# Up-projection pieces read raw in every pass, and two gate searches moved, in a one-core fp32 attention and feed-forward kernel

## The chip, the cores and the metric

The kernel runs on one core of one Trainium2 chip. The metric is the device time of one execution in microseconds (us), the median of the runs shown. Five engines take part, each with an instruction queue of its own that it works off in order: TensorE (PE, with its weight loads shown as PEld), VectorE (DVE), ScalarE (ACT), GpSimd (POOL) and SyncE (SP). In this kernel SP and POOL issue the DMAs.

## The reference

Two residual blocks over x of shape (2, 2048, 1024), all in fp32. The second is the one that matters here:

```python
x = x + attention(_layernorm(x), Wqkv, bqkv, Wo, bo)      # D = 256, one head
hs = _layernorm(x)
logits = hs @ gate_w                                       # 1024 -> 8
routing_weights, _ = jax.lax.top_k(logits, 2)
h = relu(hs @ up_w) ** 2                                   # 1024 -> 2048
shared_out = h @ down_w                                    # 2048 -> 1024
expert_out = (hs @ fc1_w) @ expert_w                       # 1024 -> 512 -> 512
moe_out = expert_out * routing_weights.sum(-1, keepdims=True)
x = x + layernorm(shared_out + moe_out @ fc2_w) * ln_gamma + ln_beta
```

## The kernel before

**Arithmetic.** Every fp32 product is made of three TensorE matmuls on a split of both operands into a rounded half ("hi", written by an ACT cast) and a remainder ("lo", written by a DVE subtract): hi·hi, lo·hi, hi·lo (`Pass3.add`, L131). The feed-forward block works on pairs of token blocks of 512 rows in four passes, b = 0 to 3 (called passes 1 to 4 here). Each pass is an "up" stage (hidden states times up_w and fc1_w) and a "down" stage (times down_w and fc2 folded with the expert weights). Each stage is done with seven Strassen-like products, p1 to p7, of ten chunks (NK = 10; chunks 0 to 7 of a product belong to up_w or down_w, 8 and 9 to the latent part). A chunk is one weight piece of 128x1024 (hi in the first 512 columns, lo in the second) and twelve matmuls.

**Order of up.** `up_order` lists the 70 chunks of a stage. In passes 2 to 4 it begins p1,0; p1,1; p2,0; p1,2; p2,1; p1,3; p2,2 ... up to chunk 19, p2,9. So chunk number m is p1,i for m = 2i-1 and p2,i for m = 2i+2, and the last is chunk 19. Then come p4, p6, p5, p3 and p7, the last in the order 0 to 5, 8, 9, 6, 7. In pass 1 the first four chunks are p1,0 to p1,3 and the mixing begins after them.

**Weight pieces.** `next_piece` runs a pipeline in program order: while chunk m is emitted, `end_piece` emits the DVE subtract of chunk m+2 (L938), `cast_piece` the ACT cast of chunk m+3 (L931), and `stage` the SP load of chunk m+4. A piece is loaded in one of three ways:

- already split, 512 KB, from a copy in HBM (`w<-w_p`, L898), with no cast and no subtract. The copy was written by POOL from an earlier pass (`w_p<-w`, L941) if `keep` was true;
- raw, 256 KB, straight from up_w or fc1_w (`raw<-in_L_ffn_up_w_dram`, L905), into a tile of the pool `spp`, which has four buffers and also holds the activations of the down stage. A raw load therefore waits for the subtract of the raw piece four loads before it;
- raw, 256 KB, from a sum of quarters or from the copy `lead` (p1,0 to p1,3) into the second half of the weight tile (`w<-wt`, `w<-wt_lead`, L905). There are seven weight tiles.

For p1 and p2 of up, `keep` is true in pass 1 for the even pieces. So passes 2 to 4 load ten of these twenty pieces split and ten raw.

**What else stands in these chunks.** After the matmuls of a chunk ACT takes the result out of PSUM (`copy` for p1 at L1239, `relu` for p2 at L1140, with a `square` over each pair at L1143). In odd chunks below 17, `out_step` finishes output rows of the pass before: on DVE `write` (L1094, L1095), on ACT `second` (L274, L275) and `first` (L262, L263), on POOL a store and an accumulating load of beta, on SP a load `res<-x` (L1078). In chunks 11, 13, 15 and 17, `split_x` prepares X["p4"]: an ACT cast `xh` (L150) and, with `split_late`, a DVE subtract `xl` (L151) that is emitted at the start of the next chunk.

**The gates.** The gate logits are summed out of products `pg` (L987), each eight matmuls appended to a chunk by `gate_part`. The first gate is complete after p2,0, the second after its product with X["p7"] in p3,8. X["p7"] is made by `split_x` in p3,1, p3,3, p3,5 and p3,7. `Gate.largest` (L1005 to L1017, DVE) searches the two largest logits of each row, `send` writes the sums to HBM and `spread` loads them back broadcast as `rwb`, both on POOL. `rwb[0]` is first used at p2,8 (L1242), `rwb[1]` at p7,8 (L1266). The small tiles `ga`, `gs`, `gtt`, `gtop`, `rwb` and the throw-away outputs `junk` of `second` and `first` come from one pool, `half`, with four buffers.

The order on every queue is the program's: the stage stands in `tc.manual_schedule()`.

Of the kernel before, what the change touches and what calls it, by code (L numbers as in the profile page):

```python
# [25 lines left out]
def kernel(  # L26
# [69 lines left out]
    def f32(t):  # L96
        return t.bitcast(FP)
# [55 lines left out]
    def flush():  # L153
        for f in late_ops:
            f()
        late_ops.clear()
# [185 lines left out]
    def piece(pr, c, n, sl):  # L342
        return tuple(v.rearrange("p (c n) -> p c n", n=n)[:, c, sl] for v in pr)
# [18 lines left out]
    def as_piece(t, s):  # L362

        return t.rearrange("p (c n) -> p c n", n=P) if s == 0 else t
# [510 lines left out]
    def direct(s, p, i):  # L875

        return s == 0 and p in ("p1", "p2", "p3") and (p, i // LEAD) != ("p1", 0)

    def source(s, p, i):
        q = RIGHT[p]  # L880
        if s == 0 and isinstance(q, tuple):
            parts = quarter(s, *q) if direct(s, p, i) else [lead]
        else:
            parts = tsum[s, q]
        t, j = (parts[0], i) if i < HU // P else (parts[1], i - HU // P)
        return t[:, ts(j, P)].rearrange("(c p) i -> p c i", p=P) if s == 0 else t[ts(j, P), :]

    def stage():


        b, s, p, i = pieces.pop(0)
        if len(pieces) < LATE and early:
            staged.append((early.pop(0), None, None))
            return
        n_w[0] += 1
        w = (wk if n_w[0] % 7 else wv).tile([P, 2 * W], FR, tag="w", name="w")
        if (s, p, i) in kept:
            nc.sync.dma_start(out=w.bitcast(FP), in_=kept[s, p, i])  # L898
            staged.append((w, None, None))
            return  # L900
        if direct(s, p, i):
            raw = spp.tile([P, 2 * W], FP, tag="sp", name="raw")[:, 0:W]
        else:
            raw = f32(w)[:, W : 2 * W]
        nc.sync.dma_start(out=as_piece(raw, s), in_=source(s, p, i))  # L905

        if s == 1 and p in ("p3", "p7", "p4"):
            keep = b == 2 and p == "p4" and i >= NK - LATE  # L910
        elif s == 0 and p in ("p1", "p2"):

            keep = b == 0 and i % 2 == 0
        else:
            keep = b == 1 or i % 2 == 0
        staged.append((w, raw, (s, p, i) if keep else None))
# [27 lines left out]
    def next_piece():  # L944

        while (pieces or staged or cast) and len(ready) < 3:
            if cast:
                end_piece()
            while pieces and len(staged) < 2:
                stage()  # L950
            if staged and not cast:
                cast_piece()
        return ready.pop(0)
# [3 lines left out]
    def acc_bank(name):  # L957
        n_bank[0] += 1
        return bank(psb if n_bank[0] % 3 == 2 else psa, name)
# [179 lines left out]
    def relu(o, v):  # L1139
        nc.scalar.activation(o, v, AF.Relu)  # L1140
# [4 lines left out]
    def relu_square(v):  # L1145
        relu(v, v)
        square(v)

    t1, later = xts, []
    with tc.manual_schedule():  # L1150
        for b in range(NBB):
# [6 lines left out]
            def h_at(name, i, n=1):  # L1158

                if i < HU // P:  # L1160
                    key, q = (name, i // 4), i % 4
                else:
                    key, q = (name in ("11", "12"), "l"), i - HU // P
                    q += 2 * (name in ("12", "21"))
                if key not in h:
                    h[key] = unit(f"h{b}", FP)
                return h[key][:, ds((q + 1 - n) * W, n * W)]
# [53 lines left out]
                nc.gpsimd.dma_start(out=gamma_sb, in_=ln_gamma.partition_broadcast(P))  # L1221
            rwb, acc = [None, None], {}
            n_bank[0] = 1
            for m, (p, i) in enumerate(UPS[b]):
                flush()
                w = next_piece()
                while later:
                    relu_square(later.pop())
                if p != "p2":
                    acc[i] = Pass3(acc_bank("pu"), NCC // 2)  # L1230
                ps = acc[i].ps
                if p == "p2":
                    acc[i].more()
                for c in range(NCC // 2):
                    acc[i].add(piece(w, c, P, slice(0, P)), piece(X[p], c, W, slice(0, W)))
                lat, pair = i >= HU // P, i % 2 and i < HU // P
                c22, c21 = h_at("22", i), h_at("21", i) if m >= 2 * NK else None
                if p == "p1":
                    nc.scalar.copy(c22, ps)  # L1239
                elif p == "p2":  # L1240
                    if lat:
                        add(h_at("11", i), ps, rwb[0], ALU.mult)  # L1242
                    else:
                        relu(h_at("11", i), ps)
                        if pair:
                            square(h_at("11", i, 2))
                elif p == "p4":
                    nc.scalar.copy(c21, ps)
                elif p == "p6":
                    add(c22, ps, c22, ALU.subtract)  # L1250
                    add(c21, c21, c22, ALU.subtract)
                elif p == "p5":
                    add(c22, c22, ps, ALU.add)
                elif p == "p3":
                    c12 = h_at("12", i)
                    add(c12, c22, ps, ALU.add)  # L1256
                    if lat:
                        add(c12, c12, rwb[0], ALU.mult)
                    elif pair:
                        relu(h_at("12", i, 2), h_at("12", i, 2))  # L1260
                        square(h_at("12", i, 2))
                else:
                    add(c21, c21, ps, ALU.add)
                    add(c22, c22, ps, ALU.subtract)
                    if lat:
                        add(c21, c21, rwb[1], ALU.mult)  # L1266
                        add(c22, c22, rwb[1], ALU.mult)
                    elif pair:
                        relu_square(h_at("21", i, 2))
                        later.append(h_at("22", i, 2))  # L1270

                if m % 2 and m < 17:
                    out_step()
                if b == 0 and m in (0, 1, 2, 3, 4, 6, 7, 8, 9, 10, 11):
                    norm2.step()
                if b == 0 and m < NB:
                    split_x(x_t[0], 1, m, X["p2"], split_late)
                if b == 0 and m % 2 == 0 and 24 <= m < 24 + 4 * NK:
                    j = m // 2 - 12
                    copy_step((1, j // NK), j % NK)  # L1280

                m4 = 10
                if m == m4:
                    x_t[1] = norm2.x
                    X["p4"] = new_x()
                if m > m4 and (m - m4) % 2 and (m - m4) // 2 < NB:
                    split_x(x_t[1], 1, (m - m4) // 2, X["p4"], split_late)
                elif m >= 2 * NK and p != "p7":
                    n = {"p4": "p6", "p6": "p5", "p5": "p3", "p3": "p7"}[p]
                    if i == 1:  # L1290
                        X[n] = new_x()
                    if i % 2 and i < 2 * NB:
                        if p == "p4":
                            sums_x(x_t, i // 2)
                        r_, f_ = PLACE[n]
                        split_x(x_t[r_], f_, i // 2, X[n], split_late)

                if (p, i) == ("p1", 0 if b else 4):
                    ga = half("ga")[:SQ, :]
                    nc.scalar.copy(ga, gate_part(X["p1"], 0))  # L1300
                elif (p, i) == ("p2", 0):
                    gs = half("gs")[:SQ, :]
                    add(gs, ga, gate_part(X["p2"], 1), ALU.add)
                    gt = Gate(gs)
                elif (p, i) == ("p4", 1):
                    add(ga, ga, gate_part(X["p4"], 1), ALU.add)
                elif (p, i) == ("p3", 8):
                    add(ga, ga, gate_part(X["p7"], 0), ALU.subtract)
                    gt = Gate(ga)
                if m == 11 or (p, i) == ("p3", 9):  # L1310
                    gt.largest()
                elif m == 12 or (p, i) == ("p7", 0):
                    gt.send()
                elif m == 14 or (p, i) == ("p7", 2):
                    rwb[p == "p7"] = gt.spread()
                if p == "p7" and (len(UPS[b]) - m) in (9, 7, 5, 3, 1):
                    step_s()
# [18 lines left out]
            for j, p in enumerate(("p1", "p2", "p6", "p5", "p3", "p7", "p4")):  # L1336
# [41 lines left out]
                if late:  # L1378
                    last_w = [next_piece() for _ in range(late)]
                    both = unit("last")  # L1380
                    while len(sp) < late:
                        i = len(sp) + len(sp_cast) - late + 2
# [78 lines left out]
```

## Time and profile before

| what | value |
|---|---|
| median of 3 runs | 2328.39 us (2327.54 to 2328.46) |
| the profiled execution: its own time | 2327.81 us |
| its span, first to last instruction | 2326.0 us |
| granted TensorE clock | 0.998 |
| PE busy | 2303.7 us, 99% of the span |
| DVE, ACT, POOL busy | 67%, 50%, 13% |
| DMA moved | 557.31 MB, mean 240 GB/s |

The profile is of one execution. A busy PE in it is a PE with a matmul in flight. The up stages of the four passes begin at about 755, 1145, 1536 and 1925 us. A list of waits names who waited for whom, the total in us, how many times, and the longest. A timeline row is: start, duration, engine, line, operation, tile written <- tiles read, count, and in brackets the idle time before it with what ended that.

### The profile page before, as it was taken

To read this page: it belongs to the slowest core of one execution; us is meant where nothing else is said; L and a number is where in the kernel's file an instruction comes from. 1 tells how busy PE (TensorE), PEld (TensorE's weight loads), DVE (VectorE), ACT (ScalarE), POOL (GpSimd) and SP (SyncE) were. 2 spreads that over 40 slices of the span, in tenths; PEclk is the share of its full clock that TensorE was granted. 3 is DMA by queue.
4 is the path that set the end of the run, shared out by engine and by line. 5 is a ranking of instruction groups with operands and counts; after the bars stand their busy time and mean duration, and the time that the engine had idled before them with its cause. 6 is when DMAs were issued, how large, how long until landed. Compare 5 with 4: busy or idle time off the path is not lost.

```text
span 2326.0 us, 28812 instructions
## 1 busy us (share of the span) xinstructions
PE 2303.7 (99%) x10332; PEld 1893.5 (81%) x10332; DVE 1550.3 (67%) x2428; ACT 1169.7 (50%) x1919; POOL 291.9 (13%) x444
## 2 busy tenths in 40 slices
PE   9999999999999999999999999999999999999998
PEld 7888888888888787888878888888888887888886
DVE  6666569888888575797555577755456675435556
ACT  6555455555543633766552474664045556214245
POOL 3222111011000111110110111110000011000000
PEclk9999999999999999999999999999999999999999
DMA  7877659799977877785877688697568579655684
GB/s 261 300 274 272 243 153 254 234 303 294 228 180 223 275 226 227 253 287 197 250 253 252 221 306 311 191 281 228 192 214 275 194 234 324 195 192 187 206 244 150
DMA packets 226942, 557.31 MB, mean 240 GB/s; under 512 B 18752, under 2 KB 89920, under 8 KB 224752
## 3 DMA queue, kind: packets, MB, share of 16 engines
q1 hardware_dynamic: 158928, 310.43, 40.0%
q0 software_dynamic: 67872, 245.05, 35.5%
q8 instruction: 82, 1.34, 0.2%
q14 instruction: 60, 0.49, 0.1%
HBM read 420.64 MB, written 185.61 MB: 261 GB/s over the span
## 4 chain that ended last, share of the span: by engine, by line
PE 87%; DMA 4%; DVE 3%; issue 3%; ACT 2%; POOL 1%; SPq 0%; DVEq 0%; POOLq 0%; ACTq 0%
PE pd L131 32%; PE pu L131 28%; PE po L131 7%; PE ps L131 7%; PE pw L131 4%; PE pq L131 4%; PE pv L447 2%; DMA raw<-in_L_ffn_up_w_dram 1%; PE pg L987 1%; PE pf L131 1%; DMA xt_d<-xblk 1%; DMA xt<-xt_d 1%; DVE xblk L214 1%; DMA raw<-in_L_ffn_fc_w_dram 0%; DVE xla L144 0%
## 5 line engine op out<-in xcount | busy, mean ns | idle before, releaser
L131 PE MATMUL pd<-w,sp 128*128 128x512 f32 x3336 | 757.7, 389 | 0.1
L131 PEld LDWEIGHTS pd<-w,sp 128*128 128x128 f32 x3336 | 626.1, 188 | 130.6 <-DVE sp L1199 0.8
L131 PE MATMUL pu<-xh,w 128*128 128x512 f32 x2240 | 691.4, 389 | 4.1 <-DVE w L938 4.1
L131 PEld LDWEIGHTS pu<-xh,w 128*128 128x128 f32 x2240 | 420.4, 188 | 94.7 <-DVE w L938 5.7
L131 PE MATMUL pu<-xl,w 128*128 128x512 f32 x1120 | 436.0, 389 | 0.0
L131 PEld LDWEIGHTS pu<-xl,w 128*128 128x128 f32 x1120 | 210.3, 188 | 44.3 <-DVE xl L151 0.3
L1194 ACT CAST sp<-h 128x512 fp32r<-128x512 f32 x238 | 146.7, 619 | 166.5 <-PE pd L131 129.0
L938 DVE TENSOR_TENSOR w<-w 128x512 fp32r<-128x512 f32 x245 | 167.7, 687 | 73.6 <-ACT w L931 68.3
L1199 DVE TENSOR_TENSOR sp<-h,sp 128x512 fp32r<-128x512 f32 x238 | 163.1, 687 | 71.3 <-ACT sp L1194 71.1
L931 ACT CAST w<-w 128x512 fp32r<-128x512 f32 x245 | 149.6, 616 | 121.2 <-DMA w<-wt 104.3
L131 PE MATMUL po<-p,v 128*128 128x512 f32 x768 | 194.3, 391 | 0.6 <-DVE p L144 0.6
L131 PE MATMUL ps<-q,k 128*128 128x512 f32 x768 | 192.3, 390 | 0.0
L131 PEld LDWEIGHTS ps<-q,k 128*128 128x128 f32 x768 | 143.7, 188 | 29.9 <-ACT max L630 0.2
L131 PEld LDWEIGHTS po<-p,v 128*128 128x128 f32 x768 | 143.0, 188 | 30.1 <-DVE p L144 1.0
L1140 ACT ACTIVATE h<-h 128x1024 f32<-128x1024 f32 x48 | 50.8, 1059 | 224.2 <-DVE h L1256 158.6
L151 DVE TENSOR_TENSOR xl<-xt,xh 128x512 fp32r<-128x512 f32 x108 | 74.4, 689 | 118.8 <-ACT xh L150 118.6
L627 ACT COPY s<-ps 128x512 f32<-128x512 f32 x128 | 74.8, 586 | 135.3 <-PE ps L131 135.2
L214 DVE STREAM_TRANSPOSE xblk<-xrow 128x1024 f32<-128x1024 f32 x60 | 120.8, 2014 | 9.4 <-ACT xrow L286 9.1
L941 POOL DMA_DIRECT2D w_p<-w x105 | 56.1, 534 | 444.5 <-DVE w L938 348.8
L632 DVE TENSOR_TENSOR max<-ps,max 128x512 f32<-128x512 f32 x120 | 82.2, 685 | 33.2 <-ACT s L627 32.3
L131 PE MATMUL pq<-xha,w_h 128*128 128x512 f32 x256 | 99.7, 390 | 0.1
L131 PE MATMUL pq<-xha,w_l 128*128 128x512 f32 x256 | 99.6, 389 | 0.0
(197 smaller groups left out, 3000.0 us busy)
## 6 DMA issues: line engine op xcount, KB each, us to landing
w<-w_p SPq DMA_DIRECT2D x260, 512.0 KB, 3.5
w<-wt SPq DMA_DIRECT2D x235, 256.0 KB, 3.3
w_p<-w POOLq DMA_DIRECT2D x105, 512.0 KB, 4.5
xt_d<-xblk POOLq DMA_DIRECT2D x56, 512.0 KB, 4.1
xt<-xt_d POOLq DMA_DIRECT2D x56, 512.0 KB, 5.6
xres<-in_L_attn_x_dram SPq DMA_DIRECT2D x32, 512.0 KB, 7.1
xres<-in_L_attn_bo_dram POOLq DMA_DIRECT2D x32, 512.0 KB, 9.7
x<-xres SPq DMA_DIRECT2D x32, 512.0 KB, 4.3
```

The source lines that it names most:

```text
L131: nc.tensor.matmul(self.ps, lhsT=a, rhs=b, start=self.i == 0, stop=self.i == self.n - 1, skip_group_check=self.on,)
L151: late_ops.append(lambda: nc.vector.tensor_tensor(lo, t, f32(hi), ALU.subtract))
L214: nc.vector.transpose(b.rearrange("p (q k i) -> p q k i", q=P // SQ, i=SQ), r.rearrange("p (k i q) -> p q k i", k=NCC, i=SQ),)
L447: nc.tensor.matmul(o, lhsT=x_, rhs=w_, start=c + i == 0, stop=c == NCC - 1 and i == 1, skip_group_check=True,)
L627: nc.scalar.copy(s["s"][k // 4][:, ts(k % 4, W)], pm)
L632: nc.vector.tensor_tensor(s["max"], pm, s["max"], ALU.max)
L931: nc.scalar.copy(w[:, 0:W], raw)
L938: nc.vector.tensor_tensor(w[:, W : 2 * W], raw, f32(w)[:, 0:W], ALU.subtract)
L941: nc.gpsimd.dma_start(out=kept[key], in_=w.bitcast(FP))
L1140: nc.scalar.activation(o, v, AF.Relu)
L1194: nc.scalar.copy(t[:, 0:W], v)
L1199: add(t[:, W : 2 * W], v, f32(t)[:, 0:W], ALU.subtract)
```

## The change

It has three parts. In the changed file the lines from L914 to L1222 have numbers one lower (the cast is L930, the subtract L937); before and after that they are the same.

1. No piece of up's p1 and p2 is kept. Pass 1 no longer writes the ten copies, and passes 2 to 4 load all twenty pieces raw.
2. The second gate's product moves from p3,8 to p3,9; its search from p3,9 to p7,0, its `send` from p7,0 to p7,1, its `spread` from p7,2 to p7,3, in every pass.
3. The first gate's search moves from chunk 11 to chunk 5 in passes 2 to 4, its `send` from 12 to 6, its `spread` from 14 to 8. In pass 1 they stay.

```diff
         elif s == 0 and p in ("p1", "p2"):
-
-            keep = b == 0 and i % 2 == 0
+            keep = False
...
             n_bank[0] = 1
+            gm = 5 if b else 11
             for m, (p, i) in enumerate(UPS[b]):
...
                 elif (p, i) == ("p4", 1):
                     add(ga, ga, gate_part(X["p4"], 1), ALU.add)
-                elif (p, i) == ("p3", 8):
+                elif (p, i) == ("p3", 9):
                     add(ga, ga, gate_part(X["p7"], 0), ALU.subtract)
                     gt = Gate(ga)
-                if m == 11 or (p, i) == ("p3", 9):
+                if m == gm or (p, i) == ("p7", 0):
                     gt.largest()
-                elif m == 12 or (p, i) == ("p7", 0):
+                elif m == gm + 1 or (p, i) == ("p7", 1):
                     gt.send()
-                elif m == 14 or (p, i) == ("p7", 2):
+                elif m == gm + 3 or (p, i) == ("p7", 3):
                     rwb[p == "p7"] = gt.spread()
```

## The prediction

> **What bounds the kernel now.** The page's first part says that PE is the bound:
>
> ```profile
> PE 2303.7 (99%) x10332; PEld 1893.5 (81%) x10332; DVE 1550.3 (67%) x2428; ACT 1169.7 (50%) x1919; POOL 291.9 (13%) x444
> ```
>
> The change removes no matmul, so it can give only places where PE stands still. Next I read the list of PE's waits. Nearly all of the feed-forward part's are two rows (total, times, longest):
>
> ```profile
> PE pu L131 <- DVE w L938: 4.1, 3, 1.5
> PE pg L987 <- ACT xh L150: 3.9, 4, 1.7
> ```
>
> Asked stage by stage, the four of `pg` are the second gate's product of each pass (1.7, 0.8, 0.7, 0.7 us) and the three of `pu` lie in p1/p2 of passes 1, 2 and 4 (1.5, 1.3, 1.3); pass 3 has none there. In the chain of waits 432 `pu` matmuls take 97.97 us, 0.227 each, while a row shows 0.39; so a listed wait costs about 0.16 more than it says: 3.9 + 4 x 0.16 = 4.5 us for `pg`, 4.1 + 3 x 0.16 = 4.6 for `pu`. All that can come back is 9.1 us. A chunk of twelve is 2.72 us, a gate product 1.84.
>
> The timelines of PE and DVE in pass 2 show the middle stall, at chunk 16 (p2,7):
>
> ```profile
> 1192.23 0.39 PE L131 MATMUL pu<-xh,w 128*128 128x512 f32 x1
> 1193.87 0.50 PE L131 MATMUL pu<-xh,w 128*128 128x512 f32 x1 [1.26 <-DVE w L938]
> ```
> ```profile
> 1183.31 0.69 DVE L938 TENSOR_TENSOR w<-raw,w 128x512 fp32r<-128x512 f32 x1 [3.05 <-ACT w L931]
> ...
> 1186.50 0.69 DVE L1005 STREAM_TRANSPOSE gtt<-gs 32x512 f32<-32x512 f32 x1
> ...
> 1189.34 0.69 DVE L151 TENSOR_TENSOR xl<-xt,xh 128x512 fp32r<-128x512 f32 x1
> ...
> 1193.13 1.29 DVE L938 TENSOR_TENSOR w<-raw,w 128x512 fp32r<-128x512 f32 x2
> ```
>
> DVE has no gap from 1183.31 to PE's release at 1193.87, and the search is 1189.34 - 1186.50 = 2.84 us of that. It started late because the raw load of chunk 12 took 15.5 us (chain of waits, from 1163.40). Pass 4 repeats this. SP and the DMA rows of pass 4 (first up stage, 1925 to 1992) say why:
>
> ```profile
> 1937.05 5.76 SPq L898 DMA_DIRECT2D w<-w_p  x2
> 1942.87 0.46 SPq L1078 DMA_DIRECT2D res<-x  x1
> 1943.37 1.18 SPq L905 DMA_DIRECT2D raw<-in_L_ffn_up_w_dram  x2
> ```
> ```profile
> raw<-in_L_ffn_up_w_dram SPq DMA_DIRECT2D x5, 256.0 KB, 14.8
> ```
>
> Two split pieces and a `res`, 1.5 MB, are issued just ahead of it, in a stretch whose DMA share is 0.93 (0.88 and 0.90 in passes 2 and 3).
>
> **Gate product a chunk later.** The last `xh` (L150) reaches PE 0.7 to 1.7 us after p3,8 ends; a chunk later it has 2.72 us more. The four stalls go: -4.5. Behind it, with T the end of p3,9: `pg` to T+1.84, DVE's sum (L1308) about T+2.1 to 2.7 (pass 3: 1702.75 to 1704.83), p7,0 ends at T+4.56, its two adds at 0.6 each, the search to T+8.8, then in passes 1 and 2 the subtract of p7,3 to T+9.5. PE wants that at T+10.2: 0.7 to spare, no cost; with the cover gone each us is one lost twice. POOL's `send` and `spread` follow; landings of 5.3 and 5.3 us (pass 1, the slowest pair) bring `rwb` to T+20, the first use is after T+22. In pass 1 ACT is without a gap from 934.57 to 952 and its ReLUs start about 0.8 later against PE; 0.3 of that I let through at the start of down. Together -4.2 (-4.5 to -2.5).
>
> **Pieces raw.** The instruction lists show 30 split loads fewer (260 to 230), 24 raw and 6 `lead` loads more, 10 POOL writes fewer, 30 casts and 30 subtracts more. Per pass that is 10 x 0.616 = 6.2 us of ACT and 10 x 0.687 = 6.9 of DVE, in 67 us of which ACT is busy 39 to 41 and DVE 34 to 37: room in the mean, not everywhere. While `out_step` runs, ACT has per four chunks (10.9 us), start to start, two each of copy (0.48), ReLU (0.5), `second` (1.47) and `first` (1.28), a square (0.98) and two casts (0.51): 9.5 us, then 10.5 with four casts. It just keeps up, and every delay there lasts. For DMA: 35 split loads fill q1 to 59.7% of 95 us (1605 to 1700), 1.62 us of all 16 engines each; 2.21 MB of raw loads, 8.4 of them, 23.9% of 32 us (768 to 800), 0.91 each. A stage of 67 us loses 10 x 0.71 = 7 of its 58 to 62 DMA us.
> [...]
> The order of issue matters more. A raw load now waits for the subtract of the raw piece four before. For chunk 12 that is the subtract of chunk 8, so it is issued at 1171.1 (worked out below) instead of 1163.4. It must land by 1178.9, where today's stall chain begins: 7.8 us. Bounds: raw loads in these stages take 7.7 to 15.9 us today; in pass 1, where all are raw, 3.0 to 9.6, median 4.3. I take pass 1's, since SP then issues nothing between `res` at 1164.8 and 1171.1: no stall, with 0.5 us in all for places not seen. The raw loads of chunks 2 to 7 have time: the buffers they take over are free while down still runs, as for the raw piece of chunk 4 today. In pass 1 ten 512 KB writes go; the stall at 805.35 hangs on a raw load of 9.6 us issued between such writes. It may go (-1.7) or stay (0): -0.8.
>
> **First search at chunk 5.** Chunk 16: DVE loses 2.84 us from the row above and gains the subtracts of chunks 14 and 15, 2 x 0.6. That is 1.6 earlier against a lateness of 1.3 + 0.16: the stalls of passes 2 and 4 go, -2.9 (0 if the load is later still).
> The new place costs. In pass 2, after chunk 3 starts at 1156.84, chunk 8 starts at 1170.47 and its second matmul wants the subtract's output at 1170.70. DVE now holds, ahead of it, the subtract of chunk 7 (cast at 1163.02), `write` and the search: free at 1164.25 + 2.65 = 1166.9. But in the instruction list the search's first transpose (L1004) waits for ACT: `gtt` gets the buffer of the `junk` that chunk 5's `second` wrote. That ran from
>
> ```profile
> 1165.71 1.15 ACT L274 ACTIVATE junk<-y,nm 128x1024 bf16<-128x1024 f32 x1
> ```
>
> and moves 0.51 back for the new cast of chunk 7: done at 1167.5 with its accumulator read. Search 1167.5 to 1170.4, subtract to 1171.1: PE is 0.43 late, 0.54 with the 0.11 that the next matmul loses after such a stall. Bounds per pass: 0 (DVE at 1166.9) to 1.9 (if `first`, 1.4 us later on ACT, is what it waits for). Three passes: +1.6. On POOL `send` and `spread` pass one store and its beta; they hold back stores that nothing in these chunks waits for. Queued behind the blocked DVE are the subtract of chunk 9, with 2 us to spare, and `write`.
>
> **Sum.** -4.2 - 2.9 - 0.8 + 1.6 + 0.5 = -5.8. The profiled execution was 2327.81 us (span 2326.0 and 1.8 around it); it becomes 2322.0. The median of the runs is 0.58 above it: 2322.6.
>
> **Rivals.** *The searches only trade places*: ACT lags at chunk 5, or the transpose waits for `first`; then chunk 8 loses 1.9 in each of three passes, 5.7 in place of 1.6: -1.7, 2326.7. For it: ACT has hardly a gap from 1159.8 to 1169.5. Against: the list names `second`. If the stalls of chunk 16 stay besides, it is 2329.6.
> *Slower: the shorter lead of raw loads.* If they still take 12.6 us (pass 2's median), each of passes 2 to 4 waits 12.6 - 7.8 = 4.8 at chunk 12, and chunk 16's stall is part of that: -4.2 - 0.8 + 1.6 + 14.4 = +11, 2339. It makes the kernel slower by over 4.7 us from 2.7 us a pass on (-5.0 + 1.6 + 3 x 2.7 = 4.7), a landing of 10.5. For it: the share of 0.88 to 0.93. Against: pass 1's 4.3.
> *It does not do what it says*: the counts above exclude that.
>
> **How the numbers follow.** The forecast has 0.56, its own range 2319.3 (all 9.1 back) to 2323.7. Trading places, or only the gate products counting (2324.2), has 0.30. The slower rival has 0.12, something unseen 0.02. The range runs to 2328.0 and leaves out the slower rival and the edge of the second case. A run of this kernel can be told from no change at about 0.2%, 4.7 us; so faster 0.58, same 0.29, slower 0.13.
>
> **What would show it.** Right: no wait of `pg` on `xh`; no wait of `pu` on the subtract at chunk 16; one of 0.2 to 1.0 us at chunk 8 of passes 2 to 4, with the transpose waiting for ACT; raw landings in p1/p2 of passes 2 to 4 near 5 us. Wrong: landings over 8 us, waits at chunks 12 to 14, or a wait of `pu` in p7.

## The result, and the profile after

The changed kernel took 2339.03 us (median of 6 runs, 2334.77 to 2341.35), the kernel before beside it 2328.19 (6 runs): a ratio of 1.0044, 95% interval 1.0034 to 1.0055. It is 10.8 us slower where 5.8 less were forecast.

The profiled execution is the fastest of the six: 2334.77 us, span 2332.6, granted clock 0.997. The page's first part and the list of PE's waits for it:

```profile
PE 2306.8 (99%) x10332; PEld 1895.1 (81%) x10332; DVE 1566.8 (67%) x2458; ACT 1184.7 (51%) x1949; POOL 287.4 (12%) x434
```
```profile
PE pu L131 <- DVE w L937: 8.4, 3, 2.8
...
PE pd L131 <- DVE sp L1198: 1.7, 2, 1.3
...
PE pu L131 <- ACT h L1239: 0.9, 1, 0.9
```

The row of `pg` is gone. The row of `pu` has again three waits, but they are twice as long and elsewhere: one at chunk 14 (p2,6) of each of passes 2, 3 and 4. The rows of `pd` and `h` are new in this size. How long each stage took, from its first matmul to the next stage's first (us):

| stage | before | after | difference |
|---|---|---|---|
| up, pass 1 | 221.40 | 217.66 | -3.74 |
| up, pass 2 | 200.38 | 201.20 | +0.82 |
| up, pass 3 | 198.82 | 204.68 | +5.86 |
| up, pass 4 | 200.43 | 201.29 | +0.86 |
| down, pass 1 | 190.52 | 191.04 | +0.52 |
| down, pass 3 | 190.40 | 192.03 | +1.63 |

The second down stage takes as long as before. With 0.65 us ahead of the first stage and in the last one this is the 6.6 us between the spans (2326.0 and 2332.6).

**The stall.** PE's timeline in pass 2, and the chain of waits that leads to the second row:

```profile
1184.24 0.39 PE L131 MATMUL pu<-xh,w 128*128 128x512 f32 x1
1187.42 0.50 PE L131 MATMUL pu<-xh,w 128*128 128x512 f32 x1 [2.78 <-DVE w L937]
```
```profile
1171.06 0.70 DVE w L937
1171.78 11.16 DMA raw<-in_L_ffn_up_w_dram
1182.96 0.62 ACT w L930
1183.58 0.49 ACT h L1239
1184.07 1.15 ACT junk L274 x2
...
1185.43 0.61 ACT xh L150
...
1186.68 0.69 DVE w L937
```

Read upwards from PE: the subtract at 1186.68 stands on DVE behind an `xl`, which waits for `xh`, which stands on ACT behind `second`, and all of ACT stood behind the cast of chunk 14's piece, which landed at 1182.96. Its load was issued at 1171.78, when the subtract of the raw piece four before it had freed the buffer. From landing to matmul it is 4.46 us, and PE wanted the piece at 1184.24 + 0.23 = 1184.47; so the load had until 1180.0, 8.2 us, and took 11.2.

**The burst.** POOL's timeline in the same stretch:

```profile
1167.69 0.54 POOL L1021 DMA_DIRECT2D rw_d<-gtop  x1 [7.85 <-DVE gtop L1016]
1169.17 0.58 POOL L1111 DMA_DIRECT2D out_dram<-y  x1 [0.95 <-issue]
1169.78 0.87 POOL L1080 DMA_DIRECT2D res<-in_L_ffn_ln_beta_dram  x1
1170.34 0.88 POOL L1025 DMA_DIRECT2D rwb<-rw_d  x1
1171.44 0.54 POOL L1111 DMA_DIRECT2D out_dram<-y  x1 [0.23 <-DVE y L1094]
1171.97 0.92 POOL L1080 DMA_DIRECT2D res<-in_L_ffn_ln_beta_dram  x1
```

`send` (L1021), emitted at chunk 6, stood 7.85 us at the head of POOL's queue until the search was done. Behind it was the store of chunk 7. In before the stores of this stretch go at 1161.19 and 1164.84, as their writes end, and `send` comes long after them:

```profile
1164.84 0.56 POOL L1112 DMA_DIRECT2D out_dram<-y  x1 [2.21 <-DVE y L1095]
...
1189.66 0.53 POOL L1022 DMA_DIRECT2D rw_d<-gtop  x1 [12.16 <-DVE gtop L1017]
```

Now two stores, two betas and the spread, 2.3 MB, are issued within 2.8 us, just ahead of and beside chunk 14's load.

**The rest of it.** The median landing of raw loads did fall. The row of pass 4's first up stage (1925 to 1990), against 14.8 us before:

```profile
raw<-in_L_ffn_up_w_dram SPq DMA_DIRECT2D x10, 256.0 KB, 5.2
```

In pass 3 the stall is followed by something else: from 1580.8 to 1585.1 PE's matmuls start 427 ns apart and not 227, and the granted clock there is 0.51. Pass 3 lost 5.9 us and passes 2 and 4 only 0.8 and 0.9, with stalls of the same size, for three reasons: the low clock cost pass 3 about 2.3 us, the wait for `h` (0.9 in the list) just ahead of its stall 1.1, and passes 2 and 4 got back the old stall of chunk 16 (1.5 each), which pass 3 never had.

### The profile page after: what moved, and what is told of

It is laid out like the page before. It is cut to its first block, busy times and chain, and to the rows that moved or that the text cites. A ratio compares the mean times of both kernels' runs of the same rounds, so it can differ in the third digit from the quotient of the medians.

```text
span 2332.6 us, 28841 instructions
## 1 busy us (share of the span) xinstructions
PE 2306.8 (99%) x10332; PEld 1895.1 (81%) x10332; DVE 1566.8 (67%) x2458; ACT 1184.7 (51%) x1949; POOL 287.4 (12%) x434
## 4 chain that ended last, share of the span: by engine, by line
PE 81%; DVE 7%; ACT 4%; DMA 4%; issue 3%; POOL 0%; DVEq 0%; SPq 0%; ACTq 0%; POOLq 0%
PE pd L131 31%; PE pu L131 27%; PE po L131 7%; PE ps L131 7%; PE pw L131 4%; DVE xblk L214 2%; DMA raw<-in_L_ffn_up_w_dram 1%; PE pg L986 1%; DMA xt_d<-xblk 1%; DVE xla L144 1%; PE pq L131 1%; PE pf L131 1%; ACT junk L274 1%; DVE w L937 1%; DVE st L179 1%
## 5 line engine op out<-in xcount | busy, mean ns | idle before, releaser
L131 PEld LDWEIGHTS pu<-xh,w 128*128 128x128 f32 x2240 | 421.5, 188 | 101.9 <-DVE w L937 10.8
L930 ACT CAST w<-w 128x512 fp32r<-128x512 f32 x251 | 153.4, 616 | 137.1 <-DMA w<-wt 115.7
L937 DVE TENSOR_TENSOR w<-w 128x512 fp32r<-128x512 f32 x251 | 171.4, 685 | 73.5 <-ACT w L930 71.6
L940 POOL DMA_DIRECT2D w_p<-w x95 | 50.8, 535 | 405.7 <-DVE w L937 316.6
L131 PE MATMUL pq<-xla,w_h 128*128 128x512 f32 x256 | 99.6, 389 | 0.0
```

The lines of the kernel that those rows point to most:

```text
L131: nc.tensor.matmul(self.ps, lhsT=a, rhs=b, start=self.i == 0, stop=self.i == self.n - 1, skip_group_check=self.on,)
L930: nc.scalar.copy(w[:, 0:W], raw)
L937: nc.vector.tensor_tensor(w[:, W : 2 * W], raw, f32(w)[:, 0:W], ALU.subtract)
L940: nc.gpsimd.dma_start(out=kept[key], in_=w.bitcast(FP))
```

## The experiments

Three parts: A raw pieces, B the gate product a chunk later, C the first search at chunk 5. Ratios are against runs of the kernel before on the same chip.

### 1. The parts apart

Theory R blames the raw loads (A), theory S the early search (C). Four kernels; the edits are against the changed kernel.

B alone:
```diff
-                keep = False
+                keep = b == 0 and i % 2 == 0
-            gm = 5 if b else 11
+            gm = 11
```


> Of the three parts only the second: the second gate product at p3's chunk 9, its search, send and spread at p7's chunks 0, 1 and 3. Every theory: the two waits of the gate product for its sums (4.5 us in the trace of before) are gone and nothing else moves, so about 2323.7 (2323.2 to 2325.5). If it is above 2327, the later search costs what the later product saves, and part two has a share in the loss of the whole.

A and B:
```diff
-            gm = 5 if b else 11
+            gm = 11
```


> Parts one and two, with the first search at chunk 11 in all passes. Theory S (the early search is the cause: its send stands in POOL's queue ahead of stores and betas and lets them go in one burst, over which chunk 14's raw load takes 11 us): the three stalls of 3.2 us at chunk 14 are gone, no raw load of passes 2 to 4 takes over 9 us, 2320 to 2324 (1.0044 goes to 0.9975). Theory R (the raw loads are the cause: a raw load waits for the subtract of four raws before it, so its lead is too short): stalls of over 2 us near chunks 12 to 16 in passes 2 to 4 stay, 2331 to 2339.

B and C:
```diff
-                keep = False
+                keep = b == 0 and i % 2 == 0
```


> Parts two and three, with half of up's first two products' pieces kept split as before. Theory S: the burst from POOL is still there and lands on a raw or split load, so at least one stall of 2 us or more in each of passes 2 to 4, 2328 to 2336. Theory R: no load is late, 2320 to 2324.

All, with the late `send`:
```diff
-                elif m == gm + 1 or (p, i) == ("p7", 1):
+                elif m == 12 or (p, i) == ("p7", 1):
                     gt.send()
-                elif m == gm + 3 or (p, i) == ("p7", 3):
+                elif m == 14 or (p, i) == ("p7", 3):
```


> The whole change, but in passes 2 to 4 the routing weights are sent and spread at chunks 12 and 14, as before; only the search itself stays at chunk 5. Theory S, in the form that POOL's send makes the burst: POOL's stores go when their writes end, chunk 14's raw load lands within 8 us, its stalls of 3.2 us are gone, 2320 to 2325. The form in which the search's work on DVE, by a later subtract and a later raw issue, makes the stall: most of it stays, 2331 to 2337. Theory R: it stays too, 2333 to 2339.

| kernel | median us | ratio, 95% interval | longest start to start of PE, chunks 12 to 16 of passes 2, 3, 4 |
|---|---|---|---|
| before | 2327.79 | 1 | 1.64, none, 1.67 |
| B | 2323.75 | 0.9983 (0.9974 to 0.9992) | 1.49, none, 1.31 |
| A + B | 2322.71 | 0.9982 (0.9973 to 0.9991) | 1.06, 0.97, 0.90 |
| B + C | 2320.98 | 0.9969 (0.9958 to 0.9981) | none |
| A + B + C, late send | 2321.02 | 0.9972 (0.9962 to 0.9983) | none |
| A + B + C | 2339.03 | 1.0044 (1.0034 to 1.0055) | 3.17, 3.30, 3.26 |

Neither theory stands alone. A over B gives -1.0 in the medians, C over B gives -2.8; the two together should have come to about 2319.9, and the whole is 19 us above that. Theory R missed with A + B, where no matmul starts more than 1.06 us after the one before and stalls of over 2 us were expected. Theory S missed with B + C: the `send` is early there too (POOL waits 7.46 us at it) and no load stalls PE. The raw rows of that kernel's pass 2 say why:

```profile
raw<-in_L_ffn_up_w_dram SPq DMA_DIRECT2D x5, 256.0 KB, 10.6
```

Its raw loads are slower in the median than the change's (6.5 in the same stretch), but only every second piece is raw, so that a buffer is reused after eight chunks and not after four: a slow load is early enough. The stall needs the short lead of A and the waiting `send` of C together.

### 2. The lead, the queue, and the change once more

Five raw buffers:
```diff
-    spp = ctx.enter_context(tc.tile_pool(name="spp", bufs=4))
+    spp = ctx.enter_context(tc.tile_pool(name="spp", bufs=5))
...
-    wk = ctx.enter_context(tc.tile_pool(name="wk", bufs=6))
+    wk = ctx.enter_context(tc.tile_pool(name="wk", bufs=5))
...
-        w = (wk if n_w[0] % 7 else wv).tile([P, 2 * W], FR, tag="w", name="w")
+        w = (wk if n_w[0] % 6 else wv).tile([P, 2 * W], FR, tag="w", name="w")
```


> The whole change with five buffers for raw pieces instead of four (and one less for split pieces, so that they fit, every sixth and not every seventh of which now takes the pool wv's single one). By now the theory is that neither part alone stalls PE: the stall needs a raw load with a short lead and POOL's burst on top of it. Then a lead longer by a chunk (2.7 us) takes that much from each of the three stalls of 3.2 us at chunk 14: 0 to 1.5 us of each stay, 2321 to 2328. Rival: the burst fills the DMA engines whoever came first, and the load lands at the same time whenever it is issued: 2334 to 2341. If the one split piece less makes waits of its own, PE waits for w elsewhere than at chunk 14.

Measured: 2324.53 us (2320.85 to 2330.27, 11 runs), ratio 0.9987 (0.9978 to 0.9996). In its profile no chunk 12 to 16 stalls at all. The burst is as in the change (POOL waits 7.84 us at `send`), so the lead decides. It does so by more than the expected 2.7 us of cover: chunk 14's load now goes out at 1170.69 of pass 2, before the first store of the burst at 1171.27, and lands after 3.3 us (4.9 and 4.6 in passes 3 and 4). The load that takes 12.4 us is chunk 15's, and PE does not stall on it. The profiled execution is its slowest, and what it lost is elsewhere, in the third down stage (198.13 us for 190.40; see experiment 3).

`send` at 6, `spread` at 14:
```diff
-                elif m == gm + 3 or (p, i) == ("p7", 3):
+                elif m == 14 or (p, i) == ("p7", 3):
                     rwb[p == "p7"] = gt.spread()
```


> The whole change with the spread of passes 2 to 4 at chunk 14; the send stays at chunk 6. Theory H (the send holds POOL's queue: a store, two betas and a store go together when it is let go): chunk 14's load still lands over 9 us after its issue and the stall is 2 to 3.2 us in each of three passes, 2330 to 2339. Rival W (the spread's own 256 KB on top of them make it): the stall is under 1 us, 2321 to 2325.

Measured: 2333.97 us (2331.5 to 2338.5), ratio 1.0028 (1.0017 to 1.0040); start to start at chunk 14 3.30, 3.30 and 1.65 us. In its chain of waits for pass 2 the load of chunk 14 is as slow as in the change:

```profile
1172.10 11.53 DMA raw<-in_L_ffn_up_w_dram
```

So the spread's 256 KB are not the cause; at most they have a share, since without them the third stall is half as long in this one profile and the median is 5 us lower. Against the kernel with the late `send`, which differs from this one only in where `send` stands (chunk 12 for 6, both with the `spread` at 14), it is 1.0028 to 0.9972 of before: `send` alone costs 13 us.

`send` at 8, `spread` at 10:
```diff
-                elif m == gm + 1 or (p, i) == ("p7", 1):
+                elif m == (8 if b else 12) or (p, i) == ("p7", 1):
                     gt.send()
-                elif m == gm + 3 or (p, i) == ("p7", 3):
+                elif m == (10 if b else 14) or (p, i) == ("p7", 3):
```


> The whole change with the send of passes 2 to 4 at chunk 8 and the spread at chunk 10: the send no longer stands in POOL's queue ahead of chunk 7's store and beta, but ahead of chunk 9's. Theory H: chunk 7's store goes when its write ends, near 1164.1 of pass 2, the burst is smaller by a store and a beta (1 MB), stall under 1 us at chunk 14, 2321 to 2325. Rival (the order doesn't matter, only that stores, betas and spread fall within the lead of chunk 14's load): 2.5 to 3.2 us each, 2333 to 2339.

Measured: 2321.96 us (2319.8 to 2324.0), ratio 0.9973 (0.9962 to 0.9983), no stall at chunks 12 to 16. POOL's timeline:

```profile
1166.31 0.56 POOL L1111 DMA_DIRECT2D out_dram<-y  x1 [5.58 <-DVE gtt L1004]
1166.89 0.86 POOL L1080 DMA_DIRECT2D res<-in_L_ffn_ln_beta_dram  x1
1168.57 0.54 POOL L1021 DMA_DIRECT2D rw_d<-gtop  x1 [0.82 <-DVE gtop L1016]
1172.33 0.58 POOL L1111 DMA_DIRECT2D out_dram<-y  x1 [3.22 <-DVE y L1094]
```

The store and beta of chunk 7 now go 2.9 us earlier than in the change (3.8 counted from the begin of the stage, which is 0.9 later here), before the search is done, and `send` waits 0.82 us. That is later than the 1164.1 expected: the row names the search's first transpose as what the store waited for. The load of chunk 14 is issued at 1172.66 and its cast starts as it lands, at 1180.35: 7.7 us in place of 11.2 (5.3 and 6.0 in passes 3 and 4, in place of 12.4 and 11.3). In the same stretch POOL's queue moves as many bytes as in the change. The DMA slices and the share of POOL's queue between 1168 and 1184, first of the change, then of this kernel:

```profile
DMA  0016999999999999899899999999999799999999
...
q0 software_dynamic: 832, 2.89, 67.4%
```
```profile
DMA  9989789677889999999999999999999899999999
...
q0 software_dynamic: 824, 2.85, 66.9%
```

In the change the engines stand idle for the first slices (0.4 us each) and have no gap after; here the same traffic starts earlier. Moving `send` behind one store and one beta, with the spread two chunks later, was worth 17 us.

The change again:

> The change itself again, for another profile of it. Its profiled execution took 2334.8 us, its others 2338.7 to 2341.4 at a lower granted clock. If the difference is the clock (in the profiled one PE ran at 427 ns a matmul instead of 227 for about 4 us after the stall of pass 3 and not after those of passes 2 and 4), an execution near 2339 shows such a stretch after two or three of the stalls, about 2.2 us each. If the difference is longer stalls, its stalls are over 4 us and the pitch stays at 227 ns.

Measured: 2339.41 us (2338.5 to 2339.7, 4 runs), ratio 1.0049 (1.0035 to 1.0063); the profiled execution 2339.19, clock 0.996. PE in pass 2, and windows of passes 2, 3 and 4 (the columns: stretch, its length, busy time and count of PE, PEld, DVE, ACT, POOL, then the granted clock, DMA share, GB/s):

```profile
1185.87 0.49 PE L131 MATMUL pu<-xh,w 128*128 128x512 f32 x1 [0.65 <-ACT h L1239]
1189.17 0.80 PE L131 MATMUL pu<-xh,w 128*128 128x512 f32 x1 [2.81 <-DVE w L937]
```
```profile
1189.17:1194.50 5.33, 5.33 (x13) 4.22 (x14) 4.90 (x7) 2.98 (x6) 0.53 (x1) 0.50 0.74 229
...
1584.85:1590.50 5.65, 5.65 (x13) 4.51 (x14) 4.89 (x7) 3.30 (x7) 0.53 (x1) 0.50 0.74 231
...
1980.50:1986.00 5.50, 5.48 (x24) 4.51 (x25) 4.92 (x7) 3.99 (x7) 0.53 (x1) 1.00 0.70 159
```

In passes 2 and 3 the clock is 0.50 after the stall and 13 matmuls take the time of 24; in pass 4 it is 1.00. Both answers were half right: the clock fell in a second pass, and the stalls of passes 2 and 3 had grown too. There the load took long enough (12.14 us in pass 2) that ACT, standing at its cast, was also late with the copy of chunk 11's result out of PSUM (L1239), and PE waited for that first: 1.03 us start to start and then 3.30. Up stage 2 took 204.8 us here and 201.2 in the first profile.

### 3. The wait for sp, and the clock

Five of the seven profiles in which the `lead` pieces are raw (the change twice, late `send`, five buffers, `spread` at 14) have a wait of `pd` for `sp` at the end of the third down stage; A + B and `send` at 8 do not. PE's waits and ACT's timeline of the kernel with the late `send`:

```profile
PE pd L131 <- DVE sp L1198: 2.3, 2, 1.9
```
```profile
1914.80 0.62 ACT L930 CAST w<-w 128x512 fp32r<-128x512 f32 x1 [7.41 <-DMA w<-wt_lead]
1915.33 0.62 ACT L1193 CAST sp<-h 128x512 fp32r<-128x512 f32 x1
```

The `lead` pieces of the next pass's p1 are raw too now; ACT stands 7.4 us at the cast of one, and the cast of `sp` for the running stage stands behind it. The next kernel keeps those two pieces split, with `send` at 8 and `spread` at 10:

```diff
-                keep = False
+                keep = b == 0 and i % 2 == 0 and not direct(s, p, i)
...
-                elif m == gm + 1 or (p, i) == ("p7", 1):
+                elif m == (8 if b else 12) or (p, i) == ("p7", 1):
                     gt.send()
-                elif m == gm + 3 or (p, i) == ("p7", 3):
+                elif m == (10 if b else 14) or (p, i) == ("p7", 3):
```


> The change with the send at chunk 8 and the spread at chunk 10 in passes 2 to 4, and two more pieces kept split: the first and third of p1, which come from the lead copy of the weights. In five profiles of kernels with raw pieces, PE waited 1.5 to 5.6 us for sp near the end of the third pass's down stage, where ACT stood 6.6 to 9.5 us at a cast for a lead piece that had not landed; it didn't in the kernels that keep them split. If those raw lead pieces are the cause: no wait of pd above 0.5 us there, 2319 to 2321.5, and the highest of its runs below 2323. Rival (the load on the DMA queues there, whatever the pieces): a wait of 1 us or more in the profile or runs above 2323, as in the kernel with the send at chunk 8 alone (2319.8 to 2324.0).

Measured: 2320.50 us (2320.3 to 2320.9, 6 runs), ratio 0.9967 (0.9955 to 0.9979), level with B + C (0.9969) and with the narrowest range of all. Its third down stage takes 190.40 us, and PE's waits in the feed-forward part have come down to one row, of the first down stage:

```profile
PE pd L131 <- DVE sp L1198: 0.3, 1, 0.3
```

Its interval overlaps that of the kernel with `send` at 8 and raw lead pieces, whose own profile had no such wait, so the times alone do not decide. The rows of ACT do:

```profile
1909.20 0.62 ACT L1193 CAST sp<-h 128x512 fp32r<-128x512 f32 x1 [0.52 <-PE pd L131]
...
1919.01 0.62 ACT L930 CAST w<-w 128x512 fp32r<-128x512 f32 x1 [8.67 <-DMA w<-wt_lead]
```

ACT still stands 8.67 us at the cast of a lead piece (9.35 in before), and that load took 12.5 us, so the traffic there is as slow as ever. But with every second lead piece split, the last cast of `sp` stands ahead of that cast and not behind it. In the seven profiles with raw lead pieces ACT stands 3.3 us (A + B) and 5.0 us (`send` at 8) at the first of these casts without a loss, and 6.3 to 9.5 us in the five that lost 1.4 to 7.7 us in this stage.

For the clock, stalls were made on purpose in the kernel B + C. ACT rewrites a chunk's weights with their own values several times before PE may use them:

```diff
+    STALL = {(0, 25): 2, (1, 14): 3, (1, 25): 4, (2, 14): 5, (2, 25): 6, (3, 14): 8, (3, 25): 10}
...
+                for _ in range(STALL.get((b, m), 0)):
+                    nc.scalar.copy(w[0], f32(w[0]))
```


> The second and third parts with split pieces (2321.0 us, no wait above 0.4 us in passes 2 to 4), and stalls made on purpose: before chunk 14 of passes 2 to 4 and chunk 25 of all passes ACT rewrites the chunk's weights in place 3, 5, 8 and 2, 4, 6, 10 times (the same values), 0.5 us each, which PE has to wait for; stalls of about 1.8 to 6 us. Theory of the clock: after a pitch of up to 3.26 us PE goes on at 227 ns a matmul, after a longer one at 427 ns for 4 to 6 us, granted clock 0.5, which costs 2.2 us or more each. Rival (the drop goes with the busy DMA queues and stores around the stall of chunk 14, not with its length): 427 ns at chunk 14 whatever the length, and none after the long stalls of chunk 25, where few transfers go.

One run: 2376.67 us, clock 0.991. The lengths differ from what was intended, since the copies also queued behind other work of ACT. Each stall, start to start, and what followed:

| pass, chunk | start to start, us | matmuls at 427 ns after it |
|---|---|---|
| 1, 25 | 2.75 | 0 |
| 2, 25 | 3.53 | 0 |
| 3, 25 | 4.83 | 13 |
| 2, 14 | 5.72 | 11 |
| 3, 14 | 7.39 | 6 |
| 4, 25 | 7.43 | 10 |
| 4, 14 | 9.72 | 12 |

```profile
1197.50:1202.20 4.70, 4.70 (x13) 3.64 (x12) 0.00 (x0) 0.00 (x0) 0.00 (x0) 0.50 0.06 23
...
1234.60:1239.00 4.40, 4.40 (x19) 3.63 (x20) 0.18 (x1) 1.31 (x3) 0.00 (x0) 1.00 0.25 83
...
1637.00:1642.50 5.50, 5.50 (x14) 4.29 (x13) 0.00 (x0) 0.57 (x2) 0.00 (x0) 0.50 0.00 0
```

The three windows follow the stalls of 5.72, 3.53 and 4.83. The rival is out: chunk 25 of pass 3 drops with a DMA share of 0.00 after it, chunk 25 of pass 2 does not with 0.25. The theory's bound of 3.26 us does not hold either, since 3.53 left the clock at 1.00. What does decide, no run here shows.

## Why the prediction was wrong, point by point

- **Gate product: right.** B alone took 4.7 us out of the four up stages (-1.4, -1.1, -0.9, -1.3) and put 0.5 into the first down stage, where 0.3 had been let through: -4.2 as in the sum, -4.0 in the medians.
- **Pass 1's stall: right in kind.** Of -0.8 with bounds -1.7 to 0 the end came true: in the kernels with raw pieces up stage 1 has no stall above 0.1 us (217.6), with split ones it keeps 1.7 to 2.3 (219.4 and 220.0).
- **Chunk 16: right.** No stall is left there in any kernel with the early search, and C over B was worth 2.8 us.
- **Chunk 8: right mechanism, too dear.** The transpose waits for ACT's `junk` as forecast (0.45 us at 1164.58 in pass 2), but PE loses 0.23 us a pass (pitches of 0.35 and 0.34) where 0.54 was taken: 0.7 in place of 1.6.
- **Raw landings: the median right, the term wrong.** The step "I take pass 1's ... no stall" priced a load by a median. Medians did fall to 5.2 to 7.0, but chunk 14's load took 11.16, 12.35 and 11.25 us in the three passes, and one load is enough. The allowance was worked out for chunk 12 alone (7.8 us), and there it was kept: chunk 12's load landed in 2.9 to 3.0 us in all three passes. For chunk 14 the allowance is 8.2, by the same working, and nothing was worked out.
- **POOL: the step that failed.** "They hold back stores that nothing in these chunks waits for" is true and not enough: what is held back comes out at once, and a load on another queue pays for it. The 2.3 MB that the step moved were counted at nothing. The runs price it: with `send` at 12 in place of 6 and nothing else moved the time falls by 13 us; with `send` at chunk 8 or 12 (and the `spread` two chunks behind it) the same kernel takes 2322.0 or 2321.0 us, inside the likeliest case's own range, and with `send` at 6 it takes 2339. That these medians lie so near the forecast of 2322.6 is in part luck, since pass 1 gave more than its term, chunk 8 cost less, and the wait for `sp`, which the sum did not have, takes some of it back in some executions.
- **The lead pieces: not seen.** Six more `lead` loads were counted, but not the cast in ACT's queue that waits for them ahead of `sp`: 1.6 and 1.4 us of the third down stage in the two profiles of the change.
- **The clock: not seen.** No stall of before is longer than 2.1 us start to start, and nothing in the sum let a stall cost more than itself. At 0.5 clock the next 11 to 14 matmuls cost 2.3 to 2.8 us more in all, once in the first profile and twice in the second.
- **The rival at 2339** hit the time by luck, with a part of the mechanism: the lead is what is too short, but it named chunk 12, a median landing of 12.6 and no clock, and stood at 0.12. Its 14.4 us of stalls are 9 in the runs; the clock and the waits for `h` and `sp`, which it did not have, came on top. What it lacked was why the landing should be slow once SP's queue is clear: POOL's queue.

By the prediction's two rows 256 KB raw, in rows of about 500 bytes (2.21 MB in 4442 packets), take 0.91 us of the engines and half of a split piece 0.81, 12% more per byte; A over B is not slower (0.9982 to 0.9983), and with `send` moved the raw kernels reach the time of the split one.

## What to carry to other kernels

An instruction moved forward in an in-order queue costs what is queued behind it (13 us here, `send` at 6 in place of 12), even if nobody waits for those transfers: ask when they will all be let go, and which load with little lead is then under way. Price a load by its slowest landing against its own allowance (12.35 us against 8.2 here), not by the median (5.2 to 7.0). Where a queue must wait for a result, put the waiting instruction behind the work whose inputs are ready first: `send` at 8 in place of 6, with the `spread` two chunks behind it, was worth 17 us here.

## What the runs showed of the hardware

After a stall of PE the granted clock can fall to 0.50. In pass 3 of the change it is 0.50 from 1578.2, inside the stall that ends at 1580.21, to 1585.0; after the stalls of passes 2 and 4 it is 1.00 (1187.4 to 1192.0 and 1975.8 to 1981.0). In the second profile it is 0.50 in the 5.33 us after the stall of pass 2 and the 5.65 us after that of pass 3, and 1.00 in the 5.50 us after that of pass 4.

The length of the stall alone does not tell. Start to start, single stalls of 3.17 and 3.26 us (the change, passes 2 and 4), 3.10 (its second profile, pass 4), 2.75 and 3.53 (the kernel with the stalls) left the clock at 1.00. Three of 3.30 with 1.03 to 1.55 just ahead (the change, pass 3; its second profile, passes 2 and 3) brought 0.50, and so did all five of 4.83 and more in the kernel with the stalls. Shorter ones can go with a lower clock too: at the end of the third down stage 3.20 with five buffers (mean clock 0.66 from 1920 to 1930) and 2.45 with 0.36 just ahead with the late `send` (0.92 and 0.91 in the two stretches of 10 us from 1910). What decides besides the length was not shown.

So of the six stalls of about 3 us in the change's two profiles three cost themselves alone and three 2.3 to 2.8 us more, and that differs from execution to execution. It is the larger part of what separates 2334.8 from 2339: up stage 2 took 3.6 us more in the second profile, some 2.6 of them by the clock.
